# Two layers of local attention: the slots at which the queries are split in their parts

## The chip, the cores and the metric

The kernel runs on one core of one Trainium2 chip. The metric is the time of one execution on the device in microseconds (us); smaller is better. Engines are named as the profile names them: PE multiplies matrices and transposes (PEld is its weight load), DVE, ACT and POOL work elementwise, SP issues transfers.

## What is computed

The input x is 4 x 2048 x 256 in float32. A pre-normalized attention block (16 heads of 16, all 2048 keys, a Gaussian prior added to the scores) comes first, then a block of two local layers whose result is added to it. The change touches the local layers alone; each is, cut to what matters:

```python
h = shift_token(x)                      # half the features from the token before
q, k, v = split(h @ wqkv)               # 8 heads of 64
q, k = rotary_xpos(l2norm(q) * qs, l2norm(k) * ksc)
o = local_attention(q, k, v)            # windows of 128: own window and the one before, masked
x = x + o @ wo
h = layernorm(shift_token(x)) * lg + lb
a, g = split(h @ w1 + b1)
x = x + (a * gelu(g)) @ w2 + b2
```

## The kernel before

**Stages.** Attention runs first, for all four batches. Then `local_layers` runs one long list of steps: a step is one (layer, batch, chunk of 128 tokens), 2 x 4 x 16 = 128 in all, and after every four chunks the feed-forward part (`glu`) is done for the group of 512 tokens. Intermediate results of a layer go to device memory and come back by transfers.

**The timetable.** A step has 32 slots (`SLOTS`). The dictionary `AT` gives each piece of a step's work the slot in which it is emitted, counted from the step's start; so pieces of three or four steps are emitted side by side, and slot 51 of one step is slot 19 of the next. The emission order is not yet the order on the engines: in this stage a scheduler arranges the instructions, engine by engine, taking the emission order as priority and its own estimate of when operands and buffers are ready. Every engine then runs its own list in order.

**A step's way through the engines.** `project` transposes the chunk (`ht`), multiplies it by the weights (`qkv_0`, `qkv_1`, `qkv_2` for queries, keys, values; helper `dense`, L409), squares queries and keys on ACT (`scale`, L1414), multiplies them with the rotary tables on DVE (L1416), sums the squares (L1421), adds the rotated half on POOL (L1429) and takes the power -1/2 of the sums on POOL (L378). `unit` scales the keys by it (L1448). `attend` then does the following:

- `turn` (L1468): four PE transposes each put the queries, tile `qt`, and the keys, tile `kt`, into a PSUM bank.
- `high_q` (L1473) and `low_q` (L1366, through the helper `low`): a float32 value is kept as two float32r parts. ACT copies the rounded high part out of the bank, DVE subtracts it from the bank's value and writes the low part. Two instructions each, one for each half of the partitions, into tile `lq` (two of them, for even and odd chunks).
- `high_k` (L1482) and `low_k` (L1366): the same for the keys, into tile `lk`. Behind each subtraction SP issues a transfer (L1488) that copies the parts to the other half of the partitions.
- `product` (L1504): scores `sim` from `lq` and `lk`, two matmuls for each head; `masked` (DVE, L1516), `weights` (ACT exponentials, L1530), `normalize` (POOL, L1541).

`gather` transposes the weights (tiles `pT`, L1563, four per step), copies them out (L1574), multiplies them by the values (`po`, L1584), projects (`lo`) and adds to the tokens (`fg`, L1614). `glu` normalizes (`hn`, L1649, transposed in `hnt`), multiplies by w1 in eleven pieces (`w1`), evicts the gates (ACT, L1693), applies the gate on DVE (`gate`, L1712) and multiplies by w2.

**PSUM.** There are eight banks of 128 x 512. Tiles named `qkv_` have two of their own; all others (`ht`, `qt`, `kt`, `sim`, `pT`, `po`, `lo`, `hnt`, `w1`, `w2`) share six, and a new tile takes a bank when the last reader of the old one is done. The bank of `qt` is held until `low_q` is done, that of `kt` until `low_k` is done.

```python
"turn": (36, 41),              # queries, keys
"parts": (51, 52, 44, 44),     # high_q, low_q, high_k, low_k
"sim": (54, 59, 62, 59),
```

Of the kernel before, what the change touches and what calls it, by code (L numbers as in the profile page):

```python
# [95 lines left out]
    "rotate": (17, 34),  # L96
    "unit": (22, 15, 41),
    "turn": (36, 41),
    "parts": (51, 52, 44, 44),
    "sim": (54, 59, 62, 59),  # L100
    "masked": (59, 59, 63, 63),
    "weights": (59, 61, 69, 70),
# [1761 lines left out]
```

## Time and profile before

| | |
|---|---|
| median of 3 runs | 5709.82 us (5705.14 to 5711.7) |
| profiled execution | 5716.1 us, its span from the first to the last instruction 5714.0 us |
| granted PE clock, mean | 0.989 |
| attention, 0 to 3040 us | PE busy 2948.0 us |
| local layers, 3040 to 5714 us | PE busy 2509.0, DVE 2180.4, ACT 1798.0, POOL 1658.6 us |
| ACT copies of the queries' high part (L1473), window 3100 to 5600 | 246, median 581 ns |
| DVE subtractions for the queries' low part (L1366), same window | 246, median 689 ns |

The window from 3100 to 5600 us holds 123 of the 128 steps. Each engine runs its list in order; time in which an engine has nothing to run is put down to the instruction that released it. Ends of matmuls in the profile are modelled.

### The profile page before, as it was taken

What the parts mean: (1) busy time and instruction counts of PE and PEld (TensorE: products, weight loads), DVE (VectorE), ACT (ScalarE), POOL (GpSimd) and SP (SyncE); (2) the same over time, 40 slices, a digit from 0 to 9 for tenths busy, and PEclk for the clock granted to TensorE, in tenths of its full rate; (3) what the DMA queues carried; (4) which work ended last, traced back from release to release, by engine and by line L of the source; (5) the groups of instructions that cost most, each with busy time, mean ns of one, the idle gap of its engine ahead of it and who ended that gap; (6) DMA issues with size and microseconds to landing.
All of it is one profiled execution on the core that took longest, in us unless ns stands there. A gap on an engine that the chain in (4) does not pass through costs nothing.

```text
span 5714.0 us, 106950 instructions
## 1 busy us (share of the span) xinstructions
PE 5457.0 (96%) x35544; PEld 3381.0 (59%) x35544; DVE 4833.2 (85%) x13769; ACT 4466.1 (78%) x9400; POOL 2181.2 (38%) x2358
## 2 busy tenths in 40 slices
PE   7999999999999999999997999999999999999998
PEld 4444444444444444444444787888887887878787
DVE  6889999889998899999985888888887888888886
ACT  3889998889988899889995667766766677666665
POOL 4221002320122200110003666666666666666665
PEclk8999999999999999999998999999999999999999
DMA  4443233433434322333213121222122322222211
GB/s 133 116 118 108 75 91 104 119 89 84 117 110 116 106 81 65 112 83 99 67 45 117 48 55 48 55 52 55 50 57 78 89 55 63 61 63 55 61 52 41
DMA packets 348758, 456.51 MB, mean 80 GB/s; under 512 B 88400, under 2 KB 212304, under 8 KB 346672
## 3 DMA queue, kind: packets, MB, share of 16 engines
q1 hardware_dynamic: 336688, 416.10, 26.4%
q0 software_dynamic: 11520, 33.58, 1.9%
q8 instruction: 285, 4.67, 0.3%
q14 instruction: 265, 2.17, 0.1%
HBM read 267.41 MB, written 105.12 MB: 65 GB/s over the span
## 4 chain that ended last, share of the span: by engine, by line
PE 59%; DVE 22%; ACT 8%; POOL 5%; issue 3%; DMA 2%; SPq 1%; DVEq 0%; POOLq 0%; ACTq 0%
PE s L870 16%; PE acc L977 16%; PE s L953 9%; PE w L409 4%; ACT sim L1530 4%; PE sim L1504 3%; POOL rn L378 3%; DVE s L884 3%; DVE lk L1366 2%; PE qkv L409 2%; PE po L1584 2%; DVE sim L1516 2%; DVE hn L1649 2%; PE pqk L409 2%; DVE tops L882 2%
## 5 line engine op out<-in xcount | busy, mean ns | idle before, releaser
L968 ACT ACTIVATE e<-s 128x512 f32<-128x512 f32 x4096 | 2153.0, 611 | 203.1 <-PE s L953 131.0
L870 PE MATMUL s<-k,q 64*128 64x512 f32 x3200 | 1284.5, 465 | 53.0 <-DVE tops L884 33.0
L884 DVE CUSTOM_DVE_ANT_0 s<-s,wide 128x512 f32<-128x512 f32 x1408 | 975.7, 694 | 182.6 <-PE s L870 171.5
L977 PE MATMUL acc<-e,v 128*32 128x512 f32 x8192 | 1096.3, 607 | 0.0
L953 PE MATMUL s<-q,k 64*128 64x512 f32 x4096 | 841.8, 419 | 17.9 <-DMA q<-rowd 11.8
L870 PEld LDWEIGHTS s<-k,q 64*128 64x128 f32 x3200 | 529.4, 185 | 491.9 <-ACT more L890 242.0
L1530 ACT ACTIVATE sim<-sim,top,rn 128x256 f32<-128x256 f32 (+1 forms) x1024 | 597.3, 586 | 259.4 <-DVE top L1522 258.9
L882 DVE TENSOR_REDUCE tops<-s 128x1 f32<-128x512 f32 x896 | 610.3, 681 | 64.3 <-PE s L870 61.2
L1541 POOL TENSOR_TENSOR sim<-sim,inv 128x512 f32<-128x512 f32 (+1 forms) x512 | 513.5, 1024 | 347.6 <-DVE inv L1538 344.5
L953 PEld LDWEIGHTS s<-q,k 64*128 64x128 f32 x4096 | 540.0, 186 | 148.6 <-ACT e L968 54.8
L894 DVE CUSTOM_DVE_ANT_0 more<-s,more 128x512 f32<-128x512 f32 x896 | 613.1, 684 | 0.0
L870 PEld LDWEIGHTS s<-kd,q 64*128 64x128 f32 x896 | 164.7, 184 | 743.3 <-DVE tops L884 374.8
L890 ACT ACTIVATE more<-s 128x512 f32<-128x512 f32 x896 | 540.0, 603 | 63.4 <-PE s L870 28.9
L409 PE MATMUL w<-gt,ww 128*128 128x512 f32 x2112 | 545.0, 397 | 3.5 <-DVE lk L1366 3.2
L964 DVE TENSOR_TENSOR s<-s,band 128x187 f32<-128x187 f32 (+2 forms) x1408 | 469.1, 354 | 78.4 <-PE s L953 77.5
L870 PE MATMUL s<-kd,q 64*128 64x512 f32 x896 | 445.9, 498 | 0.7 <-ACT more L890 0.7
L409 PEld LDWEIGHTS w<-gt,ww 128*128 128x128 f32 x2112 | 386.9, 189 | 79.1 <-issue 3.7
L1429 POOL TENSOR_TENSOR r<-r,t 128x256 f32<-128x256 f32 x512 | 367.8, 740 | 149.7 <-DVE t L1416 137.2
L1516 DVE CUSTOM_DVE_ANT_0 sim<-sim,cst 128x256 f32<-128x256 f32 (+1 forms) x1024 | 376.0, 407 | 56.4 <-PE sim L1504 53.3
L378 POOL TENSOR_TENSOR rn<-ss,nhalf 128x16 f32<-128x16 f32 x128 | 372.9, 2913 | 95.2 <-DVE ss L377 92.4
L1008 POOL TENSOR_TENSOR oall<-o,inv 128x256 f32<-128x256 f32 x64 | 39.9, 623 | 937.6 <-DVE inv L1007 900.8
L1504 PE MATMUL sim<-lk,lq 128*128 128x256 f32 (+1 forms) x2048 | 338.2, 294 | 26.9 <-DVE lq L1366 18.8
(197 smaller groups left out, 9645.8 us busy)
## 6 DMA issues: line engine op xcount, KB each, us to landing
lk<-lk SPq DMA_DIRECT2D x256, 256.0 KB
k<-sm SPq DMA_DIRECT2D x638, 64.0 KB
q<-sm SPq DMA_DIRECT2D x632, 64.0 KB
sm<-part SPq DMA_DIRECT2D x112, 256.0 KB
q<-sm SPq DMA_DIRECT2D x128, 128.0 KB
k<-sm SPq DMA_DIRECT2D x512, 32.0 KB
fg<-f SPq DMA_DIRECT2D x32, 512.0 KB
tb<-td SPq DMA_DIRECT2D x128, 128.0 KB
```

What stands on the lines that cost most here:

```text
L378: nc.gpsimd.tensor_tensor(dst, var, nhalf[:, : var.shape[1]], ALU.pow)
L409: nc.tensor.matmul(ps, a, c, start=first and k == 0 and i == 0, stop=last and k == n - 1 and i == 2,)
L870: nc.tensor.matmul(ps, q1[u // 4 % Q_BUFS][rows, u % 4 * P : (u % 4 + 1) * P], keys, start=True, stop=True,)
L882: nc.vector.tensor_reduce(top, ps, AX.X, ALU.max)
L884: nc.vector.tensor_tensor_reduce(ps, ps, prior, 1.0, LOWEST, ALU.add, ALU.max, top)
L890: nc.scalar.activation(more, pairs.pop((u, 1, half)), AF.Relu)
L894: nc.vector.tensor_tensor_reduce(more, ps, more, 1.0, LOWEST, ALU.add, ALU.max, tops[u // NC][:, chunk(u), 2 * half : 2 * half + 1],)
L953: nc.tensor.matmul(ps, k2[s // 4 % Q_BUFS][rows, kc % 4 * P : (kc % 4 + 1) * P], q2[h % 2][rows, j % 2 * QT : (j % 2 + 1) * QT], start=Tru ...
L968: nc.scalar.activation(e, sums.pop((s, j)), AF.Exp)
L977: nc.tensor.matmul(acc[32 * j : 32 * j + 32, :], vs[b, kc][:, own * VS : own * VS + 32], es_.pop((s, j)), start=kc == 0, stop=kc == NC - 1,)
L1530: nc.scalar.activation(w, w, AF.Exp, bias=m["top"][:, h : h + 1], scale=s["rn"][:, h : h + 1], accum_out=m["sums"][:, h : h + 1],)
L1541: nc.gpsimd.tensor_tensor(w, w, m["inv"][:, hs].unsqueeze(2).to_broadcast([P, 2, width]), ALU.mult)
```

## The change

Of the queries' parts, `high_q` moves from slot 51 to slot 38 and `low_q` from slot 52 to slot 39: right behind the transposes of the queries (slot 36) and ahead of those of the keys (slot 41) and of the keys' parts (slot 44). Nothing else is edited. As the scheduler decides the order, the instructions around them shift too.

```diff
     "turn": (36, 41),
-    "parts": (51, 52, 44, 44),
+    "parts": (38, 39, 44, 44),
     "sim": (54, 59, 62, 59),
```

## The prediction

> **What bounds the kernel now.** I read the table by stretches first, to find the stage the change touches. The local layers run from about 3040 us to the end.
>
> ```profile
> core 0: us, PE busy (x) PEld busy (x) DVE busy (x) ACT busy (x) POOL busy (x), PEclk, DMA share, GB/s
> 0.00:3040.00 3040.00, 2948.01 (x17805) 1278.03 (x17806) 2652.79 (x7834) 2668.10 (x5209) 522.68 (x865) 0.99 0.34 97
> 3040.00:5714.00 2674.00, 2508.98 (x17741) 2102.96 (x17739) 2180.43 (x5935) 1797.97 (x4191) 1658.57 (x1493) 0.99 0.22 61
> ```
>
> The second row is the stage: 2674 us for 128 steps, 20.9 us each, PE busy 94%, DVE 82%, ACT 67%. The same PE work must run before and after, so the time can move only by PE's idle time, 165 us of the stage (some of it at the two ends). The first 3040 us are attention; the built program is the same there. Second, therefore, PE's own waits inside the stage (window 3100 to 5600 us, which holds 123 of the 128 steps; columns: total us, times, longest):
>
> ```profile
> PE pT L1563 <- DVE lk L1366: 32.4, 66, 1.5
> PE sim L1504 <- DVE lq L1366: 18.5, 27, 1.6
> PE hnt L1664 <- DVE hn L1649: 14.9, 31, 1.1
> PE pT L1563 <- DVE lq L1366: 14.9, 29, 0.5
> PE pT L1563 <- DVE fg L1614: 12.9, 21, 1.1
> PE sim L1504 <- DMA lk<-lk: 4.6, 5, 2.3
> PE pT L1563 <- POOL sim L1541: 4.6, 7, 1.3
> PE pT L1563 <- DVE gate L1712: 4.5, 29, 0.2
> ```
>
> The pT transposes read only the weights that POOL normalized (4.6 us). Their waits for DVE's lk, lq, fg and gate, 64.7 us together, cannot be for data: they are waits for a PSUM bank that kt, qt, lo or w1 still holds. The 18.5 us of sim for lq are for data. Third, the chain of waits, to see who is late when such a bank comes free (start, us, what):
>
> ```profile
> 4037.30 0.58 ACT sq L1414
> 4037.89 0.51 ACT mid L1725
> 4038.39 0.48 ACT lk L1482
> 4038.90 0.59 ACT lk L1482
> 4039.51 0.68 DVE lk L1366
> 4040.23 0.69 DVE lk L1366
> 4040.96 0.75 DVE gate L1712
> 4041.71 0.33 DVE fg L1614
> 4042.04 0.60 DVE ss L1421
> 4042.66 0.70 DVE lq L1366
> 4043.38 0.17 DVE ss L377
> 4043.59 0.70 DVE lq L1366
> 4044.29 0.14 issue
> 4044.43 1.08 PE pT L1563 x8
> ...
> 4062.09 4.87 DMA lk<-lk
> ```
>
> The reader is to see that the queries' lower parts come last on DVE, 3 us behind the keys', though qt was transposed earlier than kt, and that PE then waits for the second of them. The last line is the transfer which the keys' parts still need before the scores can use them.
>
> **What moves.** No instruction is added or removed. Per step four instructions move: two ACT copies (L1473, 581 ns median) and two DVE subtractions (L1366 on lq, 689 ns). In the built program DVE now runs lk, lk, lq, lq in 95 of 128 steps and lq, lk, lk, lq in 32; after, it is lq, lq, lk, lk in all 128. ACT goes from 62, 32 and 34 (queries already first) to queries first in all. No DMA of the queries exists. On SP the order shifts only behind DVE: in some steps the keys' two transfers (L1488) now stand ahead of the next table load tb, which is not needed for two steps; POOL's work is unchanged, but its power (L378) waits for ss, below.
>
> *Banks.* The six banks are handed out by the order in which they come free. In layer 0, batch 2 the three tiles that wait in the chain above took, before, the banks of kt 8 (pT 7_0), w1 3 (pT 7_1) and qt 8 (pT 7_2); after, those of qt 8, kt 8 and lo 6. For pT 8 it was kt 9, lo 7, pT 8_0, qt 9, and becomes qt 9, kt 9, lo 7, pT 8_0. In the chain's times, lq would end where the Squares now keep DVE waiting, near 4039 instead of 4044.3.
>
> (a) pT for lq, 14.9 us: qt is free 3 us or more earlier; all of it goes. (b) pT for gate, 4.5: that bank is no longer asked for there; I take 3. (c) pT for lk, 32.4 in 66 waits, 0.49 each: the bank of kt is asked for one tile later, four transposes, 0.54 us by the eight in 1.08. That covers a mean wait if lk comes no later; two thirds, 21. (d) pT for fg, 12.9: add now stands ahead of lk in some steps, but these waits come at the end of a stretch (4067 to 4081 us) in which the chain is DVE without a gap, so one thing moved ahead pushes another back; one third, 4. (e) sim for lq, 18.5 in 27 waits: next late is the keys' transfer. From the trace's packets the last one lands 0.5 us before the first sim in these steps (c mod 4 = 2), so 0.5 of 0.69 can go; I take 11. Sum 54 us in the window, times 128/123: 56 us. The ends: nothing of (c) to (e) gives 19, all of (a) to (e) 87.
>
> *Prices.* On DVE, 1.38 us of lq now stand ahead of lk, and of the scaling of the next keys (L1416). What hides it is a wait that is there already:
>
> ```profile
> DVE r L1416 <- ACT sq L1414: 113.9, 93, 2.2
> ```
>
> That is 1.2 us each time, in which DVE has nothing to do until ACT has squared; lq fits in. If the wait were gone, lk would be 1.38 us later in every step. On ACT, 2 x 0.581 = 1.16 us of query copies move ahead of the Square, the gates' evictions (L1693) and the key copies in the 94 steps where they stood behind at least one: up to 94 x 1.16 = 109 us if each stood on the path, and nothing if none did. PE shows hardly a wait for what ACT frees (3.1 us of qkv for the scaling behind the Square), and in the chain of this window ACT sim (9.0%) and ACT lk (2.8%) are ACT's main lines: I take a sixth, 18 us. The scaling's delay also puts ss, POOL's power (2.91 us) and the key's unit scaling later; the transposes of the keys follow them 5 us or more later in three of four steps by the trace, so I count nothing; uncovered, it would be the same 1.2 us per step, counted in the 109 already.
>
> A rule speaks against the move. The Trainium skill, "PSUM — Partial Sum Buffer", section "PSUM bank collisions raise a hardware error", says that two engines never use the same bank and quadrant at once, ACT against DVE included, two reads as well. The row above agrees: scaling waits for the Square though both only read qkv. By that rule alone each scaling would be later by what is put ahead of its Square, and the sum would be the full 109 us of cost instead of 18. For the transfer of (e), "DMA: Bandwidth & Descriptors", section "Anatomy of one DMA — SWDGE (gpsimd) path", has about 2.0 us plus bytes over 436 GB/s for the other kind of queue, an estimate of 2.6 us for 256 KB; the chain shows 4.87 us. With 2.6 us all of (e) would be gained, 19 us instead of 11.
>
> **Sum.** 56 - 18 = 38 us less. The profiled execution took 5716.1 us (span 5714.0), 6.3 over the median of the runs, 5709.8. The change is the same for both: 5678 for such an execution, 5672 for the median.
>
> **Rivals.** *The keys pay (slower).* Place: lk on DVE, and through its transfer the scores. In steps with c mod 4 = 1 the keys' last packets land 0.9 us after the first sim has begun already, in those with 2 the slack is 0.5. If lk is the full 1.38 us later there, because ACT's query copies take the time in which DVE was waiting, PE waits 32 x 1.38 + 32 x 0.84 = 71 us more, (e) is lost, and with the 18 of ACT against 45 from (a) to (d) it is 44 us slower: 5754. It decides once lk is about 0.7 us, one subtraction, later than now in these two steps. For it: ACT lk and DVE lk are on the chain above. Against it: the wait for the Square.
> *The gain is given back (no change).* PE gets its banks earlier and then waits for data that come from the DVE stretch, 4067 to 4081; (c), (d), (e) vanish, and 19 against 18 leaves 5709, give or take 11. For it: DVE at 82% and unbroken in the chain there. Against it: pT has its data from POOL 1.2 us or more before it starts, by the medians of all four kinds of step (c mod 4).
> *All of it.* No cost and all bank waits gone: 87 us, 5623.
> That the change does not do what it says is excluded by the built order.
>
> **How the numbers follow.** This kernel's runs differ by about 0.1%; 0.2%, 11 us, is what can be told from no change. The forecast (5640 to 5698) 0.48, more than it 0.07, given back 0.16, keys pay 0.29. The given-back case is mostly within 11 us of now (0.13) with 0.03 on the fast side. Faster 0.58, same 0.13, slower 0.29. Range: 5640 leaves 0.07 below; 5752, just under the price of the slower rival, leaves 0.11 above.
>
> **What would show it.** Right: pT's waits for lq and gate gone, for lk under 15 us; sim's wait for lq gone and for DMA up to about 10; PE's busy time unchanged to 0.5%; DVE's wait for the Square below 60 us. Wrong: sim for DMA lk over 30 us (the keys pay), new waits of w1 or qkv for ACT's gates or the scaling (my 18 us is too small), or PE's waits for hn grown by what pT lost (given back).

## The result, and the profile after

The changed kernel takes 5762.32 us (median of 4 runs, 5756.95 to 5763.14) against 5710.68 us (4 runs, 5705.14 to 5711.70): ratio 1.009, 95% interval 1.0078 to 1.0102, 0.9% or some 52 us slower. The forecast was 38 us faster; its range, 5640 to 5752, does not hold the time.

The table by stretches, local layers of the kernel after, over the profiled span of 5760.0 us (columns: PE, PEld, DVE, ACT, POOL busy, granted clock, DMA share, GB/s):

```profile
3040.00:5760.00 2720.00, 2556.09 (x17698) 2117.06 (x17697) 2171.39 (x5922) 1798.70 (x4190) 1672.81 (x1492) 0.98 0.22 60
```

Read beside the row of the kernel before in the prediction: PE's idle time is the same (2720 - 2556 = 164 us, 165 before). Its *busy* time has grown by 47 us for the same matmuls. Attention, the first 3040 us, is as before.

PE's own waits after, window 3100 to 5600 us (total us, times, longest):

```profile
PE pT L1563 <- POOL sim L1541: 17.9, 11, 4.2
PE hnt L1664 <- DVE hn L1649: 16.9, 31, 1.2
PE pT L1563 <- DVE fg L1614: 16.6, 28, 1.1
PE sim L1504 <- DVE gate L1712: 16.0, 27, 1.3
PE sim L1504 <- DMA lk<-lk: 11.9, 20, 2.1
PE pT L1563 <- DVE lq L1366: 6.2, 7, 1.4
...
PE pT L1563 <- DVE lk L1366: 2.8, 2, 1.8
```

The waits of pT for lk and lq and of sim for lq, the largest before, are gone or small. In their place stand sim waiting for a gate, pT waiting for POOL's weights, and smaller new waits of qkv for `ht` (4.9 us) and the scaling (4.8).

DVE's waits, same window:

```profile
DVE rn L1447 <- POOL rn L378: 118.6, 67, 4.1
...
DVE lq L1366 <- ACT lq L1473: 58.9, 78, 0.9
DVE r L1416 <- ACT sq L1414: 58.4, 67, 2.8
```

The wait for the Square has halved, as forecast (113.9 before). DVE's wait for POOL's power grew from 67.1 to 118.6 us, by about as much, as if DVE now waited at the next place instead. And lq now waits for ACT's copies: 58.9 us, 16.2 before.

**Short waits inside the busy time.** To find the 47 us I matched the trace's matmuls with the built list and took, for each, the time from the start of the matmul before it, less the pace of that kind back to back. This "excess" needs no end of a matmul. Over the stage it grew from 178 to 229 us: 51, about the whole loss.

Behind the start-up, in the window 3250 to 5600 us, I sorted it by what released the matmul. Waits for a PSUM bank are 105.8 us before and 104.0 after, waits for data 52.1 and 54.4. So the bank waits did not shrink: those of pT fell from 86 to 34, those of the other tiles grew from 20 to 70. The rest grew by 31: no releaser shown, half-speed clock, and pairs of `po` matmuls that other tiles now break up. How these 31 us divide was not settled.

### The profile page after: what moved, and what is told of

It reads as the page before. It is cut to its first block, busy times and chain, and to the rows that moved or that the text cites. A ratio compares the mean times of both kernels' runs of the same rounds, so it can differ in the third digit from the quotient of the medians.

```text
span 5760.0 us, 106977 instructions
## 1 busy us (share of the span) xinstructions
PE 5505.0 (96%) x35544; PEld 3399.3 (59%) x35544; DVE 4826.4 (84%) x13769; ACT 4467.9 (78%) x9400; POOL 2196.6 (38%) x2358
## 4 chain that ended last, share of the span: by engine, by line
PE 61%; DVE 21%; ACT 6%; POOL 5%; issue 3%; DMA 3%; SPq 1%; POOLq 0%; DVEq 0%; ACTq 0%
PE s L870 16%; PE acc L977 15%; PE s L953 9%; PE w L409 6%; PE sim L1504 3%; ACT sim L1530 3%; PE qkv L409 3%; DVE s L884 3%; POOL rn L378 3%; PE po L1584 3%; DVE hn L1649 2%; DMA lk<-lk 2%; DVE tops L882 2%; DVE lk L1366 2%; DVE sim L1516 1%
## 5 line engine op out<-in xcount | busy, mean ns | idle before, releaser
L953 PE MATMUL s<-q,k 64*128 64x512 f32 x4096 | 841.4, 418 | 16.9 <-DMA q<-rowd 12.9
L1008 POOL TENSOR_TENSOR oall<-o,inv 128x256 f32<-128x256 f32 x64 | 39.9, 624 | 937.3 <-DVE inv L1007 901.3
```

The source lines that it names most:

```text
L953: nc.tensor.matmul(ps, k2[s // 4 % Q_BUFS][rows, kc % 4 * P : (kc % 4 + 1) * P], q2[h % 2][rows, j % 2 * QT : (j % 2 + 1) * QT], start=Tru ...
```

## The experiments

**Where the loss sits.** Two kernels give the changed slots to a part of the steps only; the steps of one part have the lists of the kernel before, those of the other the lists of the kernel after. The edit is

```diff
-                put(at, "parts", [high_q, low_q, high_k, low_k])
+                for slot_, piece in zip((38, 39, 44, 44) if (l, b) == (0, 0) and c < 8 else (51, 52, 44, 44), (high_q, low_q, high_k, low_k)): tt.put(at + slot_, piece)
```

> The early slots (38, 39) only in the first 8 steps of layer 0, batch 0, the old ones after; from then on the built order is that of before. By the ends of the products with the values, step by step, the changed kernel is 14 us behind after step 7 and 46 us at the end. Theory 'root wait' (DVE stands behind the key's unit scaling until POOL's power is there): the first steps alone cost 12 to 19 us, about 5725. Rival 'spread evenly' (ACT's query copies or the keys' transfers cost the same in each step): 8 of 128 steps, 3 us, about 5714.

> The other half: old slots in the first 8 steps, early ones after; from then on the built order is that of the changed kernel. Root wait: 27 to 36 us over before, about 5742. Spread evenly: 48 us, about 5759.

In `late_first8` the condition is the opposite one, `(l, b) != (0, 0) or c >= 8`. Measured: early in the first eight steps alone 5726.83 us (ratio 1.0024, 1.0015 to 1.0033), +15 us; early in all others 5743.88 (1.0049, 1.0032 to 1.0066), +32. Together 47 of the 52. The loss has two places: the first eight steps, and 120 steps at 0.27 us each.

**POOL's power.** DVE's wait for it was the most obvious suspect. Here a subtraction stands in place of the power of the 16 sums (queries and keys are then scaled by other numbers), in the kernel before and in the changed one; all lists stay as they are.

```diff
-        nc.gpsimd.tensor_tensor(dst, var, nhalf[:, : var.shape[1]], ALU.pow)
+        nc.gpsimd.tensor_tensor(dst, var, nhalf[:, : var.shape[1]], ALU.subtract if var.shape[1] == 16 else ALU.pow)
```

> Before, with POOL's power of the 16 sums left out: a subtraction stands in its place (the scores are scaled by other numbers). All engines' lists are the same as before. It is the base for the next run. POOL's instruction falls from 2.9 us to under 0.5, DVE's wait for it from 67 us to under 15. Root wait and rivals alike: 10 to 60 us faster than before.

> The changed kernel with the same power left out; all lists as in the changed kernel. Root wait: what the changed kernel lost is lost at this wait, so it stands at most 12 us above cheap_root_before, or below it by up to 30 (the bank waits that went). Rival 'ACT copies' (1.16 us ahead of Square and gates) and rival 'keys pay' (the keys' transfer later): both untouched by it, so it stays 35 to 55 us above cheap_root_before.

Measured: 5644.82 us (0.9879, 0.9865 to 0.9894) with the old slots, 5693.91 (0.9968, 0.9957 to 0.9980) with the new. Both gain, but the difference stays 49 us. The power is on the path and does not cause the loss; that theory ("root wait") falls. Only in the start-up does it count: there the changed slots lose 9 us between the ends of step 0 and step 7, 17 with the full power. From step 7 to the end they lose 44 us with the cheap power, 34 with the full one.

**One kind of step at a time.** From step 8 on, early only for chunks with one remainder c mod 4 (condition `((l, b) != (0, 0) or c >= 8) and c % 4 == 0`, and so on).

> From step 8 on, the queries' parts are split early only for chunks with c mod 4 = 0; all other steps keep the old slots. Theory 'end of the group' (the queries' subtractions, which have slack, stand ahead of scaling, sums, ht and copies in the layer-norm stretch at the end of each group of four, which have none): this step lies outside that stretch, -8 to +6 us. Rival 'every step pays' (ACT's query copies ahead of Square and gates wherever they are): a quarter of the 32 us of the steady part, +5 to +11.

> The same for c mod 4 = 1 alone. 'End of the group': outside the stretch, -8 to +6 us. 'Every step pays': +5 to +11 us.

> The same for c mod 4 = 2 alone, whose two subtractions then stand between the tiles of the layer norm. 'End of the group': nearly the whole steady loss is here although sim's own wait for lq (15 us) goes: +25 to +40 us. 'Every step pays': +5 to +11, or less, by the wait that goes.

> The same for c mod 4 = 3 alone, whose parts come right behind the stretch, ahead of the scaling of the next group's second chunk; pT's waits for lq and gate of this step (about 30 us) should go. 'End of the group': -15 to 0 us. 'Every step pays': +5 to +11 us.

| early for c mod 4 = | us | ratio, interval | against before |
|---|---|---|---|
| 0 | 5755.56 | 1.0079, 1.0065 to 1.0093 | +44 |
| 1 | 5707.44 | 0.9993, 0.9984 to 1.0002 | -4, not told from no change |
| 2 | 5817.91 | 1.0188, 1.0174 to 1.0201 | +107 |
| 3 | 5693.82 | 0.9969, 0.9958 to 0.9981 | -17 |

Neither theory of the expectations holds. The four sum to +130 where all together cost +32, so they do not add. But the even remainders pay and the odd ones do not. The trace of the kernel before shows a difference that fits. DVE, at the keys' parts for chunks 11 (remainder 3) and 12 (remainder 0); the number in brackets is the idle time ahead and its releaser:

```profile
3934.70 0.69 DVE L1416 TENSOR_TENSOR r<-qkv,tb 128x512 f32<-128x512 f32 x1 [2.21 <-ACT sq L1414]
3935.31 0.68 DVE L1416 TENSOR_TENSOR t<-qkv,tb 128x512 f32<-128x512 f32 x1
...
3937.04 1.41 DVE L1366 TENSOR_TENSOR lk<-kt,lk 64x512 fp32r<-64x512 f32 x2 [0.47 <-ACT lk L1482]
```

```profile
3957.13 0.68 DVE L1416 TENSOR_TENSOR r<-qkv,tb 128x512 f32<-128x512 f32 x1
3957.72 0.68 DVE L1416 TENSOR_TENSOR t<-qkv,tb 128x512 f32<-128x512 f32 x1
3958.47 1.41 DVE L1366 TENSOR_TENSOR lk<-kt,lk 64x512 fp32r<-64x512 f32 x2
3959.91 0.75 DVE L1712 SCALAR_TENSOR_TENSOR gate<-w,b,gate 128x512 f32<-128x512 f32 x1
```

In the first, DVE idles 2.21 us ahead of the scaling; two subtractions of lq (1.38 us) put there cost nothing. In the second it has no gap; they push lk and the gate back. By the chunk being scaled (window 3250 to 5600), DVE waited for the Square 58.3 us in 29 steps for remainder 0, 39.9 in 28 for remainder 2, 8.8 in 29 for 1, and 1.6 in two steps for 3. The scaling beside lq of remainder 3 is that of remainder 0, and so on: lq of 0 and 2 meet hardly a gap. With 3 early the 58.3 us become 0.3. With 1 early the gap stays (41.2 us), but DVE's list only trades there: one subtraction moves ahead of lk and one scaling behind it. The price is to be seen in lk: median us from the end of kt to the end of the second subtraction for lk.

| kernel | c mod 4 = 0 | 1 | 2 | 3 |
|---|---|---|---|---|
| before | 4.51 | 3.54 | 5.83 | 2.67 |
| early for 0 | 4.90 | 4.60 | 5.83 | 2.66 |
| early for 1 | 4.51 | 3.55 | 5.83 | 2.67 |
| early for 2 | 2.86 | 3.54 | 7.37 | 7.77 |
| early for 3 | 4.03 | 3.54 | 5.83 | 2.66 |
| after | 4.51 | 3.19 | 7.38 | 3.05 |

Early for 1 or 3, no step's lk is later. Early for 0, lk of remainder 1 is 1.06 us later, and the pT that takes the bank of that kt waits 33 us more in its 29 or so turns: 1.1 us each. Early for 2, its own lk is 1.54 later; and in that order the key's unit scaling, which waits for POOL's power, stands ahead of lk of remainder 3, which comes 5.1 us later and holds the bank that w1's first piece takes:

```profile
PE w L409 <- DVE lk L1366: 70.0, 23, 3.2
```

In that run PE's half-speed stretches behind 3040 us add up to 138 us (56 before), one in nearly every group of four chunks; half of the difference, 41 us, is the most that the clock can have taken. 20 of 22 such waits of 3.1 to 3.2 us have a half-speed stretch that begins within 1.5 us of their end. The Trainium skill, "TensorE: Matmul & The Clock Gate", section "HAM oscillation — how this bites in real kernels", has PE fall to half its clock when it idles for more than some 3.4 us. From start to start of the matmuls these gaps are 3.54 us, so this trace stands at the edge of the rule. The trace of `bankkt_after`, further down, does not agree: there a half-speed stretch begins within 1.5 us of the end of 21 of 27 waits of only 2.2 us.

**Adding the kinds of step.**

> From step 8 on, the queries' parts are split early for chunks with c mod 4 = 1 and 3, the others keep the old slots. If the phases' effects add (-4 and -17 alone): 5688 to 5694, that is -17 to -23 us. If a new handing-out of the banks decides each combination anew, any value between -25 and +40.

> From step 8 on, early for all chunks but those with c mod 4 = 2; on PE the list is that of early for c mod 4 = 1 and 3. Theory 'end of the group' (with c mod 4 = 2 the subtractions stand between the layer norm and the scaling: the waits of qkv 0 and 1, po 1, sim 3 and hnt that the changed kernel and c mod 4 = 2 alone share, some 40 us): those waits are gone, -25 to 0 us against before. Rival 'banks' (each order hands the banks out anew, and c mod 4 = 0 alone cost 44 us by w2 behind a gate and pT behind lk): +20 to +45 us.

> As the changed kernel from step 8 on, but for c mod 4 = 2 the parts stand at slots 45 and 46: DVE runs lk, lk, the scaling of the next chunk, lq, lq, the sum of squares, instead of lq, lq, lk, lk, scaling, sum. 'End of the group': the waits of qkv for ht and the scaling are mostly gone, sim's wait for lq stays away: -25 to +5 us. If the price is at the sum, ht and copies that still stand behind lq: +10 to +30.

> As early for c mod 4 = 1 and 3, in the first eight steps too. If the start-up's 15 us (inv behind unit on DVE, PE's clock at half for several windows more) come from each early step there: half of them, +5 to +9 us against the kernel that is early for odd chunks from step 8 on; if they come from the even chunks' place in the list: 0 to +3 us.

The conditions are `c % 2` and `c % 4 != 2` from step 8 on; `early_2at45` has (45, 46, 44, 44) for remainder 2, else as the changed kernel from step 8 on; `early_odd_all` has `c % 2` for all steps. Measured: 5697.16 us (0.9977, 0.9967 to 0.9987), 5742.11 (1.0055, 1.0042 to 1.0068), 5832.41 (1.0212, 1.0198 to 1.0226) and 5699.34 (0.9980, 0.9971 to 0.9989). `early_odd` misses the sum of its parts by 3 us, and `early_2at45` lies 90 us and more above both of its ranges. With `late_first8` this is a ladder from before to after:

| step | us | difference |
|---|---|---|
| before | 5710.7 | |
| early for 1 and 3, from step 8 | 5697.2 | -13.5 |
| and for 0 | 5742.1 | +44.9 |
| and for 2 | 5743.9 | +1.8 |
| and in the first eight steps | 5762.3 | +18.4 |

So the "end of the group" theory, that remainder 2 pays, falls: once 0 is early, 2 costs nothing more. Between the first two rungs PE's list is the same in the group of chunks compared; DVE has two subtractions elsewhere, ACT's order shifts with them, and the banks are handed out anew: the second tile pT of remainder 3 takes the bank of kt instead of the fourth piece of w1, and w2 takes that piece's bank instead of the bank of lo. The waits with 0 early as well (`early_not2`):

```profile
PE pT L1563 <- DVE lk L1366: 45.4, 41, 1.7
PE w L409 <- DVE gate L1712: 31.6, 27, 1.3
```

With 1 and 3 alone (`early_odd`) the second line does not appear, and the first is

```profile
PE pT L1563 <- DVE lk L1366: 11.3, 23, 1.7
```

Counted from start to start and by position, w2 loses 38.9 us (the gate that frees its new bank is late) and pT of remainder 0 34.2 (lk of the next chunk, 1.08 us later: 4.61 against 3.53); 18.9 and 7.4 are won at pT of remainder 3. Net this is 47 us, the whole difference of 45. Slots 45 and 46 for remainder 2 were meant to be harmless and cost most: the unit scaling again came ahead of lk of remainder 3, which ends 8.11 us behind kt. And early for 1 and 3 in the first eight steps as well adds 2 us, so the start-up's loss, too, comes only once the even steps are early.

What happens in the start-up is plain in the trace of after, DVE and POOL (start, us):

```profile
3159.07 0.17 DVE L1447 TENSOR_SCALAR rn<-rn 128x8 f32<-128x8 f32 x1 [4.01 <-POOL rn L378]
...
3159.75 0.17 DVE L1538 RECIPROCAL inv<-sums 128x4 f32<-128x4 f32 x1
```

```profile
3156.12 2.91 POOL L378 TENSOR_TENSOR rn<-ss,nhalf 128x16 f32<-128x16 f32 x1
3160.00 2.04 POOL L1541 TENSOR_TENSOR sim<-sim,inv 128x512 f32<-128x512 f32 x2 [0.96 <-DVE inv L1538]
```

The reciprocal of the second half of the weights stands behind the unit scaling in DVE's list, which waits for POOL's power; POOL then waits for the reciprocal, and pT for POOL (17.9 us in the stage's window, 4.6 before; `early_first8` has 17.1 in the window's first 200 us alone). PE's clock adds to it: four half-speed stretches, 23.9 us in all, between 3130 and 3210 us in `early_first8` and four as long in the changed kernel; none there before. Half of that, 12 us, is the most that the clock can have taken of the start-up's loss.

**The banks.** Is it the order on DVE, or the handing out of banks? Here kt gets a bank of its own, and five are shared by the rest; DVE's subtractions keep their places, but for one of lq of remainder 3, which with the old slots now stands ahead of lk.

```diff
-            pp, pq = pool("fp", 6, space=PSUM), pool("fpq", 2, space=PSUM)
+            pp, pq, pt = pool("fp", 5, space=PSUM), pool("fpq", 2, space=PSUM), pool("fpt", 1, space=PSUM)
...
-                banks = pq if name.startswith("qkv_") else pp
+                banks = pq if name.startswith("qkv_") else pt if name.startswith("kt_") else pp
```

> The kernel before, with the keys' transposes kt in a PSUM bank of their own and five banks instead of six shared by the rest. Its lists differ from those of before in a few places. No theory fixes its own time within 20 us; it is the base for the next kernel.

> The changed kernel with the same separate bank for kt; on DVE the queries' and keys' subtractions stand as in the changed kernel. Theory 'order on DVE' (the queries' subtractions stand ahead of work without slack): against the kernel before with the separate bank it stays 40 to 55 us slower. Theory 'banks' (the waits removed at pT come back at other tiles because the shared banks are handed out anew): the difference moves by more than 20 us, to any side.

> Early only for c mod 4 = 3 from step 8 on, with the separate bank for kt. 'Order on DVE': 17 us under the kernel before with the separate bank, as with the shared banks (within 8). 'Banks': the gain of 17 us came from pT 0 not waiting for the bank of kt (11 of it), which a separate bank takes out: -8 to +10 us.

Measured: 5762.64 us (1.0093, 1.0079 to 1.0107) with the old slots, 5835.50 (1.0220, 1.0206 to 1.0234) with the new, 5744.18 (1.0057, 1.0043 to 1.0071) with remainder 3 alone early. The separate bank, which leaves five to the rest, costs 53 us by itself. The new slots now cost 73 us instead of 52: above what "order on DVE" expected, and 21 is just over the line I had set for "banks", so this does not decide between them. The clock blurs it further: half-speed stretches are 78 us with the old slots and 155 with the new, so up to 38 of the 73 can be the clock's. Remainder 3 gains 18 again although the wait for the bank of kt, to which "banks" had put its gain, cannot occur. Its gain goes with the filled gap on DVE: the scaling of remainder 0 waits 11.6 us for the Square there, 73.9 with the old slots (window 3250 to 5600). What the other steps' delay costs depends on the tile that meets it: with the new slots the largest wait here is

```profile
PE sim L1504 <- DVE gate L1712: 60.8, 28, 2.2
```

(45.3 with the old ones). I read the two theories as two halves of one: DVE's order makes a release late, the banks say who waits. All runs fit this, but none shows one half without the other.

**A faster version.** The power is on the path, so it is split in halves, the eight keys' sums first; `unit` then scales the keys before it takes the queries' half.

```diff
-                    inverse_root(m["rn"], m["ss"], 1e-24, ALU.max)
+                    nc.vector.tensor_scalar(m["ss"], m["ss"], 1e-24, None, ALU.max)
+                    for half in (slice(LH, 2 * LH), slice(0, LH)):
+                        nc.gpsimd.tensor_tensor(m["rn"][:, half], m["ss"][:, half], nhalf[:, :LH], ALU.pow)
```

> A try at a faster version: early for c mod 4 = 3 alone from step 8 on, and POOL's power (2.9 us for 16 sums) split in two halves of 8, the keys' ahead of the queries', so that DVE's scaling of the keys waits for half a power only. DVE waited 101 us for that power in the kernel with c mod 4 = 3 early; a power cheap on all sums gave 66 us. If a third of that comes: 5665 to 5680; if POOL's two instructions cost more than the wait: 5690 to 5720.

> The kernel before with POOL's power split in two halves, the keys' first; the queries' parts at the old slots. If the 26 us of the version with c mod 4 = 3 early come from both edits (17 from the early parts, the rest from the halves): 5696 to 5706. If the halves alone bring them: 5680 to 5690.

> The power in halves, and the queries' parts early for c mod 4 = 1 and 3 from step 8 on. With the whole power, adding c mod 4 = 1 to 3 made 3 us of difference or none: 5680 to 5692.

Measured: halves alone 5693.94 us (0.9972, 0.9962 to 0.9981); with remainder 3 early 5683.68 (0.9953, 0.9940 to 0.9965); with 1 and 3 early 5681.42 (0.9951, 0.9939 to 0.9964). The first try, `keys_first_c3`, came 4 us above the range it was to reach. Halves alone came 2 us under the range for a gain from both edits; they bring 17 us, and the early parts 10 to 13 more. The last is the fastest of the kernels that compute the same results, 29 us under before; by 2 us it is not told from the one with remainder 3 alone.

## Why the prediction was wrong

**The bank terms came true line by line, and were given back at other tiles.** From the same lines of the profile, window 3100 to 5600: (a) pT for lq 14.9 to 6.2, 8.7 won, not all of 14.9; (b) the wait for the gate gone, 4.5 for the 3 taken; (c) pT for lk 32.4 to 2.8, 29.6 won for the 21 taken; (d) pT for fg grew from 12.9 to 16.6, where 4 were to be won; (e) sim's wait for lq has left the list and the wait for the transfer grew from 4.6 to 11.9, 11 net, for the 11 taken. With the sign of (d) wrong the sum is still 50, for the 54 forecast. That (e) is 11 to the microsecond is luck: 0.5 of 0.69 of 18.5 us is 13. For (e) the estimate of 2.6 us from the Trainium skill, "DMA: Bandwidth & Descriptors", section "Anatomy of one DMA — SWDGE (gpsimd) path", which is for the other kind of queue, would have given 19; the trace's own packets came nearer. But these lines are not the sum: over all tiles PE waited for banks as long as before (105.8 and 104.0 us).

**The step that failed is the price.** The prediction put DVE's 1.38 us for lq at nothing: "What hides it is a wait that is there already ... 1.2 us each time ... lq fits in." 1.2 us is a mean over 93 waits of all kinds of step. Sorted by the kind, the wait is 2.0 us beside lq of remainder 3, 1.4 beside that of 1, 0.3 beside that of 0 and next to none beside that of 2. Half of the moves had no cover, and the prediction itself had what that costs: "lk would be 1.38 us later". It measured 1.55 for remainder 2 in the changed kernel, 1.06 for the chunk behind remainder 0 where that is early alone. By the sum of the prediction, 56 won and 52 lost make a price of 108 us; I had taken 18. From start to start some 100 of it can be placed: 50 us of waits for banks at other tiles, 31 without a releaser, 2 for data, 17 in the start-up. That 108 is near the upper end of 109 is chance, since that end was ACT's.

What ACT's copies cost alone was not measured: no run moves high_q without low_q. The rival stands, since the steps in which both copies pass the key copies on ACT are those of remainders 0 and 2, the steps that pay. The waits speak against a large share: PE's waits put down to ACT are 3.3 us in all (1.0 before), lk waits 8.0 us for ACT's key copies (23.7 before), and the scaling's wait for its Square has grown in no kind of step. Only the lq subtractions wait longer for ACT, 18 us of it at remainder 0, where DVE had no gap.

**"The time can move only by PE's idle time" was a wrong reading.** PE's idle time did not change, its busy time took the loss. The Trainium skill, "Perfetto Trace Analysis", section "Tensor Engine Instruction (MATMUL, LD_WEIGHTS)", says that a matmul's end is estimated and not observed; the 47 us agree. A wait shorter than the modelled rest of a matmul counts as busy: in the kernel before, a transpose is drawn 273 ns long, and back to back the next one starts 109 ns after it.

**"I count nothing" for ss, POOL's power and the unit scaling** was wrong in the start-up, where the reciprocal stands behind it, and where remainder 2 is early alone. In the steady part of the changed kernel the test with a cheap power shows it right: the difference stayed.

**The rivals.** "The keys pay" forecast 5754 (with its slack of 0.5 us the second term of its sum is 0.88 and not 0.84, 1 us more), and its trigger came for remainder 2 (lk 1.55 us later, 0.7 needed), but for remainder 1 lk is 0.35 earlier, and its path, the transfer, took 7 us, not 71: near in time, by another road. "The gain is given back" named the mechanism that happened, PE having its banks and waiting for the next late thing, but with its loss at the price of its gain; hn grew by 2 us only. What it missed is that the banks, handed out anew, put other tiles behind late readers.

Of my signs, pT for lk under 15 and DVE's wait for the Square under 60 came true, and sim for DMA nearly (11.9 for about 10), beside a slower kernel; PE's busy time unchanged to 0.5% did not (1.9% more). They showed what went, not what came.

What stays open: how much of the 45 us of remainder 0 is the two subtractions' delay and how much the new banks, since no run here moves the one without the other; what ACT's copies alone cost; and what the 31 us without a releaser are.

## What to carry to other kernels

When work is moved into an engine's idle time, sort that idle time by the kind of step first: a mean wait covers nothing in the steps that have none, and here moving the same two instructions was worth -17 us in one of four steps and +107 in another. Banks that are handed out in order of release make each removed wait a new assignment, so count all waits for banks together, before and after, and try the move one kind of step at a time. Where an engine's ends are modelled, compare start to start.

## What was not expected of the hardware

PE's busy time rose by 47 us for the same matmuls. PE's half-speed stretches come in multiples of 3.4 us and follow small changes of the waits: 56 us in the layers before, 89 after, 138 with remainder 2 alone early; in `bankkt_after` they begin behind waits of 2.2 us. The power on POOL costs 1.64 us for 128x8 and 2.91 us for 128x16, so two halves cost 0.37 us more than the whole and still gained 17 us.
